# Turning over adjacency masks in a graph attention kernel: transposing transfers within SBUF in place of TensorE transposes and copies

## The chip, the cores and the metric

The kernel runs on one core of one Trainium2 chip. The metric is device time in microseconds (us) from the first to the last instruction; a kernel's time is the median of its runs. The profile shows one execution, on the engines TensorE (PE; its weight loads are listed as PEld), VectorE (DVE), ScalarE (ACT), GpSimd (POOL) and SyncE (SP, which here only issues transfers).

## The reference: what is computed

Two layers of graph attention over 32 graphs of 512 nodes with 512 features each. `adj` is an integer matrix of 512 x 512 per graph.

```python
# layer 0
h = relu(layernorm(x))
scores = leaky_relu(h@w_src [:, None] + h@w_dst [None, :] + b, 0.2)
scores = where(adj + eye == 0, -inf, scores)
x = x + softmax(scores, axis=-1) @ h                    # over the row of a node
# layer 1: two GAT layers, the first with 4 heads of 256, then elu, the second with 1 head of 512
h = relu(layernorm(x))
mask = (adj > 0) | eye
xl = (h @ W).reshape(B, N, H, F)
e = leaky_relu(asrc[:, :, None] + adst[:, None, :], 0.2)
attn = softmax(where(mask[..., None], e, -1e9), axis=1)  # over the column of a node
out = einsum('bsdh,bshf->bdhf', attn, xl) + bias
x = x + out
```

Everything is float32, and the masks are exact in bfloat16: an entry is 0 where there is an edge and -2^100 where there is none.

## The kernel before

A graph needs each of its two masks both ways: `m0` and its transpose `m0T` for layer 0, `m1` and `m1T` for the two attention layers of layer 1. One way is used by DVE to take the largest masked score of a row, the other is added to the scores by POOL ahead of the exponential. In layer 1 the maxima read `m1T` and the addition reads `m1`; in layer 0 the maxima read `m0` and the addition reads `m0T`.

```python
def edge_weights(kind, scores, a_of, c_of, mask_max, mask, junk_of=None):
    a_row = spread("m_row", scores + mask_max(*ROW), a_of, AHEAD)     # 4 TensorE transposes
    amax, z, m = Buffer("col"), Buffer("col"), Buffer("col")
    for t in range(T):                                                 # T = 4 blocks of 128 nodes
        def largest(t=t):
            nc.vector.tensor_tensor_reduce(                            # L480
                junk[...], mask_max.at[:, t, :], a_row.at, 1.0, LOWEST, ALU.add, ALU.max,
                accum_out=amax.at[:, t : t + 1])
        op("DVE", on_dve(N), largest, a_row(*ROW) + mask_max(t), amax(t))
    # ... cut: m from amax (L486, L488); m_row and c_row spread by TensorE (L417)
    for t in range(T):
        # ACT: E = Prelu(c_row + a)        L498
        # DVE: E = E - m_row               L501
        # POOL: E = E + mask               L503
        # ACT: E = exp(E)                  L506
    return E
```

The transposition of a mask, for which TensorE and a bfloat16 identity are used; a transpose lands in PSUM (kind "acc", four places), and ACT or DVE copies it to SBUF:

```python
def transposed_mask(m, mT, ahead):
    for k in range(T):
        pt = Buffer("acc")
        view = lambda pt=pt: pt.at[:, : N // 2].bitcast(BF16)
        for t in range(T):
            pe_transpose(                                              # L417
                ahead, pt, lambda t=t, view=view: view()[:, node_block(t)], m(t) + mT("place"),
                lambda t=t, k=k: m.at[:, t, node_block(k)], ident_b, t)
        evict(pt(*ROW), mT(k), view, lambda k=k: mT.at[:, k, :], N)    # L450 on ACT or L456 on DVE
```

Where the masks come from (`masks0` does the same for `m0`, with other comparisons), and the buffers concerned. There is one place for each of `adj`, `m0`, `m0T`, `m1` and `m1T`:

```python
def masks1(b):
    a, m1, m1T = load_adj(b), Buffer("m1"), Buffer("m1T")              # load on POOL's queue, L552
    op("DVE", ..., lambda: nc.vector.tensor_scalar(m1.at, a.at, 0.0, NO_EDGE, ...))    # L593
    for t in range(T):
        op("DVE", ..., lambda: nc.vector.tensor_mul(m1.at[:, t, own], ..., off_diag))  # L599
    transposed_mask(m1, m1T, AHEAD)
```

The products that project the features (L717) accumulate in PSUM places "sums" (two) and "acc" (four), and ACT or DVE copies or DVE adds (L450, L456, L730) the results to SBUF. The aggregation (L516) multiplies the weights E with the values.

All of this is laid out before the run by a planner: `op(engine, cost, emit, reads, writes, ahead)` records an operation, with how long it holds its engine and when its result is there (both in ns, as estimates written into the kernel), and `plan.run()` plays the operations through and emits them engine by engine in the order that comes out. Each engine then works in this fixed order. The estimates of the operations touched here:

```python
def on_pe(n, dtype=F32, transpose=False):
    if transpose:
        return (110.0, 300.0) if dtype == F32 else (68.0, 220.0)
    ...
def evict(...):  # ACT: n / 1.2 + 80 ns; DVE: n / 0.96 + 70 ns
```

The main loop, per graph b: masks and projection of layer 1, the end of graph b - 1, the four heads, layer 0 of the next graphs:

```python
for b in range(B + 1):
    if b < B:
        masks1(b)
        layer1_project(b)
    if b:
        load_back(b - 1)
        layer2_out(b - 1)
    # ... cut: load_x(b + 2)
    for h in range(H):
        Es.append(layer1_scores(b, h))        # edge_weights with m1T for the maxima
        # ... cut: layer1_head for the head before
    # ... cut: layer0_out(b + 1), layer1_in(b + 1), layer0_scores(b + 2) with masks0, layer2_project(b)
plan.run()
```

Of the kernel before, what the change touches and what calls it, by code (L numbers as in the profile page):

```python
# [9 lines left out]
F32 = mybir.dt.float32  # L10
BF16 = mybir.dt.bfloat16
# [4 lines left out]
P = 128  # L16
# [18 lines left out]
class Plan:  # L35
# [11 lines left out]
    def op(self, engines, cost, emit, reads=(), writes=(), ahead=0, lock=None):  # L47


        i = len(self.ops)  # L50
        after = set()
        for buf, part in reads:
            after.update(buf.wrote.get(part, ()))
        for buf, part in writes:
            after.update(buf.wrote.get(part, ()))
            after.update(buf.read.get(part, ()))
        bufs = []
        for buf, part in (*reads, *writes):
            if buf.kind is not None and buf not in bufs:
                bufs.append(buf)  # L60
                buf.left += 1
                if buf.left == 1 and buf.kind in self.turns:
                    self.turns[buf.kind].append(buf)
        for buf, part in reads:
            buf.read.setdefault(part, []).append(i)
        for buf, part in writes:
            buf.wrote[part] = [i]
            buf.read[part] = []
        after.discard(i)
        self.ops.append((engines if isinstance(engines, tuple) else (engines,), cost, emit, after, bufs, i - ahead, lock))  # L70
# [89 lines left out]
                    known(j)  # L160


def on_pe(n, dtype=F32, transpose=False):
    if transpose:
        return (110.0, 300.0) if dtype == F32 else (68.0, 220.0)
    one = 2 * max(0.8376 * n + 2, 110.0)
    return one, one + 170.0


def on_dve(n, speed=1.0, scaled_psum=False):  # L170
    one = n / 0.96 / speed + (130.0 if scaled_psum else 70.0)
    return one, one + 85.0


def on_act(n, per_partition=0):

    one = n / 1.2 + (80.0, 140.0, 280.0)[per_partition]
    return one, one + 60.0


def on_pool(n, narrow=False):
    one = 2.04 * n + 70.0 if narrow else 2.2 * n + 100.0
    return one, one + 30.0
# [3 lines left out]
def kernel(  # L187
# [24 lines left out]
    nc = tc.nc  # L212
    B, N, D = x.shape
    H, F = att_src1.shape
    HF = H * F
    T = N // P
# [8 lines left out]
    const = ctx.enter_context(tc.tile_pool(name="const", bufs=1))  # L225
# [9 lines left out]
    def node_block(t: int) -> slice:  # L235
        return slice(t * P, (t + 1) * P)
# [34 lines left out]
    op = plan.op  # L271


    ident = const.tile([P, P], F32, name="ident")
    make_identity(nc, ident)
    ident_b = const.tile([P, P], BF16, name="ident_b")
    nc.vector.tensor_copy(ident_b, ident)
    off_diag = const.tile([P, P], BF16, name="off_diag")
    nc.vector.tensor_scalar(off_diag, ident, 0.0, None, op0=ALU.is_equal)
    minus_half = const.tile([P, T], F32, name="minus_half")  # L280
# [131 lines left out]
    ROW = range(T)  # L412

    def pe_transpose(ahead, dst, dst_of, src, src_of, identity, part):

        dtype = BF16 if identity is ident_b else F32
        op("PE", on_pe(P, dtype, True), lambda: nc.tensor.transpose(dst_of(), src_of(), identity), src, dst(part), ahead)  # L417

    def layernorm(X):

# [25 lines left out]
    def evict(src, dst, src_of, dst_of, n, bias=None, psum_half=False):  # L446

        def by_act():
            if bias is None:
                nc.scalar.copy(dst_of(), src_of())  # L450
            else:
                nc.scalar.activation(dst_of(), src_of(), AF.Identity, bias=bias)  # L452

        def by_dve():
            if bias is None:
                nc.vector.tensor_copy(dst_of(), src_of())  # L456
            else:
                nc.vector.tensor_scalar(dst_of(), src_of(), -1.0, None, op0=ALU.add)

        op(("ACT", "DVE"), (on_act(n, bias is not None), on_dve(n)), (by_act, by_dve), src, dst)  # L460

    def spread(kind, part, col_of, ahead):

        row = Buffer(kind)
        for t in range(T):
            pe_transpose(
                ahead, row, lambda t=t: row.at[:, node_block(t)], part, lambda t=t: col_of(t).to_broadcast([P, P]), ident, t
            )
        return row

    AHEAD = 400

    def edge_weights(kind, scores, a_of, c_of, mask_max, mask, junk_of=None):

        a_row = spread("m_row", scores + mask_max(*ROW), a_of, AHEAD)
# [3 lines that stand above are left out]
                count[0] += 1  # L479
                nc.vector.tensor_tensor_reduce(  # L480
                    junk[count[0] % 2], mask_max.at[:, t, :], a_row.at, 1.0, LOWEST, ALU.add, ALU.max,
                    accum_out=amax.at[:, t : t + 1],
                )
            op("DVE", on_dve(N), largest, a_row(*ROW) + mask_max(t), amax(t))
        c_all = lambda: c_of(None)
        op("DVE", on_dve(T), lambda: nc.vector.tensor_add(z.at, c_all(), amax.at), scores + amax(*ROW), z(0))  # L486
        op(
            "DVE", on_dve(T), lambda: nc.vector.scalar_tensor_tensor(m.at, z.at, SLOPE, z.at, op0=ALU.mult, op1=ALU.max),  # L488
            z(0), m(0),
        )  # L490

        E = Buffer(kind)
        m_row = spread("m_row", m(0) + E("place"), lambda t: m.at[:, t : t + 1], AHEAD)
        c_row = spread("c_row", scores + E("place"), c_of, AHEAD)
        for t in range(T):
            op(
                "ACT", on_act(N, 1),
                lambda t=t: nc.scalar.activation(E.at[:, t, :], c_row.at, AF.Prelu, bias=a_of(t), scale=1.0, alpha=SLOPE),  # L498
                c_row(*ROW) + scores, E(t),
            )  # L500
            op("DVE", on_dve(N), lambda t=t: nc.vector.tensor_sub(E.at[:, t, :], E.at[:, t, :], m_row.at), m_row(*ROW) + E(t), E(t))  # L501
            op(
                "POOL", on_pool(N, True), lambda t=t: nc.gpsimd.tensor_add(E.at[:, t, :], E.at[:, t, :], mask.at[:, t, :]),  # L503
                E(t) + mask(t), E(t), lock=True,
            )
            op("ACT", on_act(N), lambda t=t: nc.scalar.activation(E.at[:, t, :], E.at[:, t, :], AF.Exp), E(t), E(t))  # L506
        return E
# [44 lines left out]
        op("POOL", (2200.0, 8000.0), lambda: nc.gpsimd.dma_start(a.at, node_tiles(adj, b)), (), a(0))  # L552
        return a

    def transposed_mask(m, mT, ahead):
        for k in range(T):
            pt = Buffer("acc")
            view = lambda pt=pt: pt.at[:, : N // 2].bitcast(BF16)
            for t in range(T):
                pe_transpose(  # L560
                    ahead, pt, lambda t=t, view=view: view()[:, node_block(t)], m(t) + mT("place"),
                    lambda t=t, k=k: m.at[:, t, node_block(k)], ident_b, t,
                )
            evict(pt(*ROW), mT(k), view, lambda k=k: mT.at[:, k, :], N)

    def masks0(b):


        a, m0, m0T, d = load_adj(b), Buffer("m0"), Buffer("m0T"), Buffer("d")
        op(  # L570
            "DVE", on_dve(T * N, 4.0),
            lambda: nc.vector.tensor_scalar(m0.at, a.at, 0.0, NO_EDGE, op0=ALU.is_equal, op1=ALU.mult),
            a(0), m0(*ROW), lock=True,
        )
        for t in range(T):
            own = node_block(t)
            op("DVE", on_dve(P), lambda t=t, own=own: nc.vector.tensor_add(d.at[:, t, :], a.at[:, t, own], ident), a(0), d(t), lock=True)
            op(
                "DVE", on_dve(P),
                lambda t=t, own=own: nc.vector.tensor_scalar(  # L580
                    m0.at[:, t, own], d.at[:, t, :], 0.0, NO_EDGE, op0=ALU.is_equal, op1=ALU.mult
                ),
                d(t), m0(t), lock=True,
            )
        transposed_mask(m0, m0T, AHEAD)
        return m0, m0T

    def masks1(b):

        a, m1, m1T = load_adj(b), Buffer("m1"), Buffer("m1T")  # L590
        op(
            "DVE", on_dve(T * N, 4.0),
            lambda: nc.vector.tensor_scalar(m1.at, a.at, 0.0, NO_EDGE, op0=ALU.is_le, op1=ALU.mult),  # L593
            a(0), m1(*ROW), lock=True,
        )
        for t in range(T):
            own = node_block(t)
            op(
                "DVE", on_dve(P), lambda t=t, own=own: nc.vector.tensor_mul(m1.at[:, t, own], m1.at[:, t, own], off_diag),  # L599
                m1(t), m1(t), lock=True,  # L600
            )
        transposed_mask(m1, m1T, AHEAD)
        M[b] = (m1, m1T)

    slots["d"] = places("d", 1, [P, T, P], BF16)
# [311 lines left out]
```

## Time and profile before

| | |
|---|---|
| time, median of 3 runs | 3947.34 us (3946.77 to 3950.04) |
| span of the profiled execution | 3948.1 us, mean granted TensorE clock 0.993 |
| busy: PE, DVE, ACT, POOL | 98%, 74%, 43%, 37% |
| DMA | 178.36 MB, mean 45 GB/s |
| time per graph in the steady part | some 120 us |

The page gives the busy time of each engine, the chain of work that ended last, and the groups of instructions by line. A group's line reads: line, engine, operation, output <- inputs by the program's names, shapes, count | busy us in total, mean ns of one | us that the engine sat idle just before them, and what ended that idle time. Matmuls are pipelined, so the mean time of one is longer than its share of TensorE's time. A float32 matmul shows up as two matmuls. A line of the view of waits reads: who <- waited for whom: us in total, times, longest. A line of the timeline reads: start in us, length in us, engine, line, operation, output <- inputs, shapes, how many are merged.

### The profile page before, as it was taken

The page shows a single profiled execution, that of the slowest core. Times are in us where ns is not written, and L with a number is a line of the kernel's source. Part 1 is how long each engine was busy: PE and PEld are TensorE (multiplying, and loading weights), DVE is VectorE, ACT ScalarE, POOL GpSimd, SP SyncE. Part 2 cuts the span into 40 slices and gives each one's busy share as a digit, 9 for nine tenths or more (in the row PEclk, how much of TensorE's full clock was granted, in tenths as well). Part 3 has the DMA queues.
Part 4 walks back from the last instruction along what each step waited for, and adds up shares of the span by engine and source line. Part 5 has one row for each costly group of instructions (what it writes and reads, how often), then busy time and mean ns, then how long its engine had stood idle before and what let it go on. Part 6 is the DMA issues. An engine that isn't in the chain of part 4 may idle for free.

```text
span 3948.1 us, 54741 instructions
## 1 busy us (share of the span) xinstructions
PE 3860.7 (98%) x20224; PEld 3342.0 (85%) x20224; DVE 2926.7 (74%) x7733; ACT 1715.3 (43%) x2991; POOL 1478.0 (37%) x1306
## 2 busy tenths in 40 slices
PE   4899999999999999999999999999999999999998
PEld 3788888888888888888888888888888888888887
DVE  6887767777777777777777677777777777777764
ACT  2444444444444454444444444444444544444432
POOL 3434333344333343343343433443343433433421
PEclk8999999999999999999999999999999999999999
DMA  4011111111111111111111111111111111111100
GB/s 136 6 54 54 33 49 49 33 54 52 30 49 54 33 54 33 49 49 33 54 54 33 47 50 33 54 44 37 49 48 39 54 33 49 49 33 54 49 22 22
DMA packets 107421, 178.36 MB, mean 45 GB/s; under 512 B 3728, under 2 KB 40592, under 8 KB 107152
## 3 DMA queue, kind: packets, MB, share of 16 engines
q1 hardware_dynamic: 72064, 138.42, 9.5%
q0 software_dynamic: 33792, 33.56, 5.4%
q8 instruction: 158, 2.59, 0.3%
q10 hardware_dynamic: 1296, 2.88, 0.2%
q14 instruction: 111, 0.91, 0.1%
HBM read 141.30 MB, written 67.11 MB: 53 GB/s over the span
## 4 chain that ended last, share of the span: by engine, by line
PE 96%; DVE 2%; DMA 1%; POOL 1%; issue 1%; ACT 0%; SPq 0%; DVEq 0%; ACTq 0%; POOLq 0%
PE acc L516 45%; PE sums L717 22%; PE acc L717 17%; PE acc L417 6%; PE m_row L417 4%; PE c_row L417 2%; DVE junk L307 1%; POOL E_one L503 1%; DMA w<-in_L_gnn_W_dram 0%; DVE E_one L501 0%; ACT E_one L506 0%; DVE junk L480 0%; DMA x<-in_x_dram 0%; DMA w_T<-in_L_gnn_W_dram 0%; DVE w_T L399 0%
## 5 line engine op out<-in xcount | busy, mean ns | idle before, releaser
L516 PE MATMUL acc<-pair,E 128*128 128x257 f32 x4096 | 913.2, 380 | 0.0
L503 POOL TENSOR_TENSOR E<-E,m 128x512 f32<-128x512 f32 x512 | 577.6, 1157 | 825.3 <-DVE E L501 818.3
L516 PEld LDWEIGHTS acc<-pair,E 128*128 128x128 f32 x4096 | 769.2, 189 | 119.2 <-ACT pair L452 5.5
L516 PE MATMUL acc<-h,E_one 128*128 128x256 f32 (+1 forms) x2048 | 501.6, 384 | 6.3 <-ACT E_one L506 3.9
L791 ACT ACTIVATE e<-v,minus_one 128x512 f32<-128x512 f32 x256 | 184.7, 722 | 717.8 <-DVE v L782 682.4
L516 PE MATMUL acc<-xl,E_one 128*128 128x257 f32 (+1 forms) x2048 | 479.5, 381 | 2.7 <-ACT E_one L506 2.7
L480 DVE CUSTOM_DVE_ANT_0 junk<-m1T,m_row 128x512 bf16<-128x512 bf16 x640 | 411.1, 682 | 51.5 <-PE m_row L417 50.9
L506 ACT ACTIVATE E<-E 128x512 f32<-128x512 f32 x512 | 323.6, 632 | 229.6 <-POOL E L503 227.8
L516 PEld LDWEIGHTS acc<-xl,E_one 128*128 128x128 f32 x2048 | 378.6, 190 | 51.8 <-ACT E_one L506 3.1
L516 PEld LDWEIGHTS acc<-h,E_one 128*128 128x128 f32 x2048 | 367.1, 191 | 55.6 <-ACT E_one L506 13.8
L501 DVE TENSOR_TENSOR E<-E,m_row 128x512 f32<-128x512 f32 x512 | 330.3, 679 | 14.7 <-PE m_row L417 12.2
L498 ACT ACTIVATE E<-c_row,pair 128x512 f32<-128x512 f32 x512 | 314.6, 690 | 48.6 <-PE c_row L417 47.7
L717 PE MATMUL acc<-w_T,E 128*128 128x257 f32 (+1 forms) x1024 | 268.1, 384 | 14.7 <-DVE x L534 14.7
L794 DVE SCALAR_TENSOR_TENSOR v<-e,v 128x512 f32<-128x512 f32 x256 | 177.7, 694 | 138.8 <-ACT e L791 134.6
L534 DVE SCALAR_TENSOR_TENSOR x<-acc,r,x 128x256 f32<-128x256 f32 x512 | 244.8, 479 | 46.3 <-PE acc L516 43.7
L717 PE MATMUL sums<-w_T,E 128*128 128x257 f32 (+1 forms) x1024 | 271.6, 381 | 0.0
L717 PE MATMUL acc<-w,E 128*128 128x257 f32 (+1 forms) x1024 | 264.6, 381 | 0.0
L503 POOL TENSOR_TENSOR E_one<-E_one,m0T 128x512 f32<-128x512 f32 x128 | 146.5, 1176 | 309.8 <-DVE E_one L501 309.8
L506 ACT ACTIVATE E_one<-E_one 128x512 f32<-128x512 f32 x256 | 161.3, 630 | 232.1 <-POOL E_one L503 228.9
L782 DVE SCALAR_TENSOR_TENSOR v<-acc,r,b_r 128x256 f32<-128x256 f32 x512 | 246.2, 481 | 13.7 <-DVE r L779 0.4
L779 DVE RECIPROCAL r<-acc 128x1 f32<-128x1 f32 x512 | 83.5, 163 | 214.1 <-PE acc L516 211.5
L503 POOL TENSOR_TENSOR E_one<-E_one,m 128x512 f32<-128x512 f32 x128 | 144.3, 1160 | 234.1 <-DVE E_one L501 234.1
(123 smaller groups left out, 6750.1 us busy)
## 6 DMA issues: line engine op xcount, KB each, us to landing
x<-in_x_dram SPq DMA_DIRECT2D x32, 1024.0 KB, 5.1
adj<-in_adj_dram POOLq DMA_DIRECT2D x64, 512.0 KB, 5.8
spill<-x SPq DMA_DIRECT2D x32, 1024.0 KB, 4.3
x<-spill SPq DMA_DIRECT2D x32, 1024.0 KB, 5.7
out_dram<-x SPq DMA_DIRECT2D x32, 1024.0 KB, 4.3
w<-in_L_gnn_W_dram SPq DMA_DIRECT2D x6, 256.0 KB, 9.0
w<-in_L_gnn_W_dram SPq DMA_DIRECT2D x8, 127.5 KB, 4.9
w_T<-in_L_gnn_W_dram SPq DMA_DIRECT2D x4, 128.5 KB, 5.8
```

What stands on the lines that cost most here:

```text
L417: op("PE", on_pe(P, dtype, True), lambda: nc.tensor.transpose(dst_of(), src_of(), identity), src, dst(part), ahead)
L480: nc.vector.tensor_tensor_reduce(junk[count[0] % 2], mask_max.at[:, t, :], a_row.at, 1.0, LOWEST, ALU.add, ALU.max, accum_out=amax.at[:, t ...
L498: lambda t=t: nc.scalar.activation(E.at[:, t, :], c_row.at, AF.Prelu, bias=a_of(t), scale=1.0, alpha=SLOPE),
L501: op("DVE", on_dve(N), lambda t=t: nc.vector.tensor_sub(E.at[:, t, :], E.at[:, t, :], m_row.at), m_row(*ROW) + E(t), E(t))
L503: "POOL", on_pool(N, True), lambda t=t: nc.gpsimd.tensor_add(E.at[:, t, :], E.at[:, t, :], mask.at[:, t, :]),
L506: op("ACT", on_act(N), lambda t=t: nc.scalar.activation(E.at[:, t, :], E.at[:, t, :], AF.Exp), E(t), E(t))
L516: lambda s=s: nc.tensor.matmul(acc.at[:, :n], E.at[:, s, node_block(t)], of(s), start=(s == 0), stop=(s == T - 1)),
L534: lambda acc=acc, r=r, f=f, t=t: nc.vector.scalar_tensor_tensor(X.at[:, t, f], acc.at[:, :HD], r.at, X.at[:, t, f], op0=ALU.mult, op1=ALU. ...
L717: lambda k=k: nc.tensor.matmul(acc.at[:, :width], at[a]()[:, k, node_block(r)], weight_of(w, k, c), start=(first and k == 0), stop=(k == n ...
L782: lambda t=t, acc=acc, r=r: nc.vector.scalar_tensor_tensor(v.at[:, t, :], acc.at[:, :F], r.at, b1_r[:, h * F : (h + 1) * F], op0=ALU.mult, ...
L791: op("ACT", on_act(2 * F, 1), lambda e=e, ts=ts: nc.scalar.activation(e.at, v.at[:, ts, :], AF.Exp, bias=minus_one), parts, e(0))
L794: lambda e=e, ts=ts: nc.vector.scalar_tensor_tensor(v.at[:, ts, :], e.at, 1.0, v.at[:, ts, :], op0=ALU.min, op1=ALU.max),
```

## The change

The transposes of both masks are made by transposing transfers from SBUF to SBUF, issued on SyncE's queue, four for each mask. Transfer t reads the block of 128 rows t of the mask, 128 x 512 in bfloat16 (128 KB), and writes the column strip t of all four blocks of the transpose. TensorE's bfloat16 transposes, their copies out of PSUM and the bfloat16 identity are dropped. The aim is to free TensorE, and ACT and DVE, of work that a transfer can do.

Since each transfer writes a strip across all blocks, the maxima for one row block, and likewise the addition by POOL, now depend on all four transfers. The planner is told that a transfer holds the queue for 100 ns and lands after 3500 ns.

```diff
-def on_pe(n, dtype=F32, transpose=False):
+def on_pe(n, transpose=False):
     if transpose:
-        return (110.0, 300.0) if dtype == F32 else (68.0, 220.0)
+        return 110.0, 300.0
 ...
-    ident_b = const.tile([P, P], BF16, name="ident_b")
-    nc.vector.tensor_copy(ident_b, ident)
 ...
-            op("DVE", on_dve(N), largest, a_row(*ROW) + mask_max(t), amax(t))
+            op("DVE", on_dve(N), largest, a_row(*ROW) + mask_max(*ROW), amax(t))
 ...
-                E(t) + mask(t), E(t), lock=True,
+                E(t) + mask(*ROW), E(t), lock=True,
 ...
-    def transposed_mask(m, mT, ahead):
-        for k in range(T):
-            pt = Buffer("acc")
-            view = lambda pt=pt: pt.at[:, : N // 2].bitcast(BF16)
-            for t in range(T):
-                pe_transpose(
-                    ahead, pt, lambda t=t, view=view: view()[:, node_block(t)], m(t) + mT("place"),
-                    lambda t=t, k=k: m.at[:, t, node_block(k)], ident_b, t,
-                )
-            evict(pt(*ROW), mT(k), view, lambda k=k: mT.at[:, k, :], N)
+    def transposed_mask(m, mT):
+        for t in range(T):
+            op(
+                "SP", (100.0, 3500.0),
+                lambda t=t: nc.sync.dma_start(mT.at[:, :, node_block(t)], m.at[:, t, :], transpose=True),
+                m(t), mT(t),
+            )
```

More of the change, by code (lines that the diff above doesn't have):

```diff
@@ L414, in pe_transpose @@
     def pe_transpose(ahead, dst, dst_of, src, src_of, identity, part):
-        dtype = BF16 if identity is ident_b else F32
-        op("PE", on_pe(P, dtype, True), lambda: nc.tensor.transpose(dst_of(), src_of(), identity), src, dst(part), ahead)
+        op("PE", on_pe(P, transpose=True), lambda: nc.tensor.transpose(dst_of(), src_of(), identity), src, dst(part), ahead)
     def layernorm(X):
@@ L584, in masks0 @@
             )
-        transposed_mask(m0, m0T, AHEAD)
+        transposed_mask(m0, m0T)
         return m0, m0T
@@ L601, in masks1 @@
             )
-        transposed_mask(m1, m1T, AHEAD)
+        transposed_mask(m1, m1T)
         M[b] = (m1, m1T)
```

## The prediction

> **What bounds the kernel now.** I read the busy shares first, then the chain that ended last, to see whether the busiest engine is also the one that sets the end.
>
> ```profile
> PE 3860.7 (98%) x20224; PEld 3342.0 (85%) x20224; DVE 2926.7 (74%) x7733; ACT 1715.3 (43%) x2991; POOL 1478.0 (37%) x1306
> ...
> PE 96%; DVE 2%; DMA 1%; POOL 1%; issue 1%; ACT 0%; SPq 0%; DVEq 0%; ACTq 0%; POOLq 0%
> ```
>
> TensorE is both. So an instruction taken off TensorE is worth its place in TensorE's queue, and one taken off VectorE (DVE) or ScalarE (ACT) is worth nothing by itself, unless TensorE was waiting for it. The view of waits for TensorE shows how little it waits:
>
> ```profile
> PE m_row L417 <- DVE col L488: 18.3, 3, 14.2
> PE acc L417 <- DVE m L580: 18.0, 3, 16.4
> PE acc L717 <- DVE x L534: 14.7, 1, 14.7
> ```
>
> The longest single waits (14.2, 16.4 and 14.7 us) make up most of each sum, so they are events of the start and the end, not of the 120 us that each of the 32 graphs takes in between. Next the instructions that the change removes, by group:
>
> ```profile
> L417 PE MATMUL acc<-ident_b,m 128*128 128x128 bf16 x1024 | 78.0, 220 | 19.1 <-DVE m L580 18.0 <-DVE x L534 0.7 <-ACT m1T L450 0.3
> L450 ACT COPY m0T<-acc 128x512 bf16<-128x512 bf16 x67 | 35.4, 579 | 9.2 <-PE acc L417 9.2
> L450 ACT COPY m1T<-acc 128x512 bf16<-128x512 bf16 x65 | 34.9, 589 | 37.2 <-PE acc L417 35.4
> L456 DVE COPY m1T<-acc 128x512 bf16<-128x512 bf16 x63 | 25.5, 423 | 28.0 <-PE acc L417 28.0
> L456 DVE COPY m0T<-acc 128x512 bf16<-128x512 bf16 x61 | 24.1, 417 | 14.8 <-PE acc L417 14.8
> ```
>
> 1,024 transposes (32 graphs x 2 masks x 16 blocks), 132 copies on ACT, 124 on DVE. Last, how the turned mask m1T is used in one steady graph; this is the timeline of all engines from 1546 us on:
>
> ```profile
> 1546.16 0.62 DVE L599 TENSOR_TENSOR m<-m,off_diag 128x128 bf16<-128x128 bf16 x4
> ...
> 1546.68 0.83 PE L417 MATMUL acc<-ident_b,m 128*128 128x128 bf16 x12
> ...
> 1547.35 1.09 PE L717 MATMUL sums<-w_-T,hT 128*128 128x258 f32 x4
> ...
> 1550.50 0.69 DVE L480 CUSTOM_DVE_ANT_0 junk<-m1T,m_row 128x512 bf16<-128x512 bf16 x1 [1.31 <-PE m_row L417]
> ...
> 1559.13 3.38 POOL L503 TENSOR_TENSOR E<-E,m 128x512 f32<-128x512 f32 x3 [12.11 <-DVE E L501]
> ```
>
> The mask is finished at 1546.8 us, turned over by 1549.2, and first read by DVE at 1550.5 (row maxima of head 0). So the consumer comes 3.7 us behind the mask: that is the deadline which a transfer has to meet.
>
> **What the Trainium skill says.** "VectorE: DVE Perf Modes", section "The three transpose paths", puts a 128x128 bf16 transpose at 390 ns on TensorE and 1309 ns on the DMA crossbar. On TensorE the trace has 220 ns for one and, as worked out below, one each 56 ns in a row, so the page's time is one of latency; whether its 1309 ns is latency or rate no run here shows yet, and the two readings are my rivals. "Advanced Engine Details and Errata", section "X-Bar Transpose (TRN2)", says transposing transfers are as fast as others (350 to 400 GB/s); "DMA: Bandwidth & Descriptors", section "Latency and other measured facts", has 261 GB/s where the middle dimension isn't contiguous, which is the case in this destination. The kernel before has no such transfer. "TensorE: Matmul & The Clock Gate", section "Part 4: PE-mode transpose", says that the result lands in PSUM and needs a copy: the trace agrees (the 256 copies above).
>
> **The change, part by part.**
>
> *Removed from TensorE.* Not the busy time of 78.0 us: the last matmul's pipeline tail lies under the next one. The cost is start to start. In the lines above the first of 12 transposes starts at 1546.68 and the next product at 1547.35: 0.67 / 12 = 56 ns. The same difference over all the runs of transposes between 120 and 3660 us gives 55.4 us for 944, over the last 32 1.8 us. The first 48 lie in the start, where TensorE is idle two thirds of the time and they cost nothing. Gain: **57 us**. The 18.0 us of waiting in front of the transposes isn't gained: 16.4 of it is the very first wait, at 16.4 us, and the next TensorE work waits for DVE until 21.4 us anyhow.
>
> *Removed from ACT and DVE.* 70 us of ACT and 50 us of DVE, and 8 uses of the four "acc" PSUM places per graph. TensorE hardly waits for either in the steady part, so I put 0 there. In the start (60 to 120 us) DVE is busy 58.4 of 60 us; six of its copies at 0.42 us are some **2 us**.
>
> *Added.* 256 transfers of 128 KB on SyncE's queue, 33.5 MB in all beside 178 MB now; the DMA engines have a share of 11 to 15%, so bandwidth is no matter. SyncE issues four transfers per graph today (a store, a load, a store, a load), and holds 0.36 us for one; ordinary 1 MB transfers land in 4.3 to 5.7 us.
>
> *What becomes late.* m0T isn't pressed: m0 is done at 1567.6 us and m0T is read at 1650.8, 83 us later. m1T is: the maxima for row block 0 read one column strip from each of the four transfers, so the first of them waits for the last transfer. The kernel's own planner lays out all queues before the run; it takes a transfer to hold SyncE for 100 ns and to land after 3500 ns. Four then land by 0.3 + 3.5 = 3.8 us after the mask, and with signals and the m_row transposes it puts the first maximum some 4.7 us after the mask (before: 3.7). The engines work in that fixed order. If the transfers land later, DVE stands at that maximum, with the copies and additions behind it that empty PSUM for TensorE's products.
>
> *How much of such a stall reaches TensorE.* A product of four matmuls takes 0.87 us; TensorE has 6 PSUM places, and its next product into the same place waits for the copy. I estimate that it runs on for about two products, 2 us. DVE can't catch up soon: between 1552 and 1563.5 us it is busy 11.43 of 11.5. So each us of stall beyond 2 costs about 1 us, times 32. The chain behind the maxima itself has room: head 0's weights are ready 17 us after the mask and first used at 33.6.
>
> So: time = 3947 - 57 - 2 + 32 x max(0, landing - 4.7 - 2) + a little at the start, where SyncE also issues the weights.
>
> **The rivals.**
>
> A, *hidden*: 1309 ns is mostly latency, and a transfer behaves like the others, 0.4 us of SyncE each. Four land in 4 to 5 us. 3947 - 59 + 2 = **3890**. For it: the low DMA share, and the planner's 3.5 us, which was probably taken from a run, since its 5.5 us for the x load lies near the measured 5.1. Weight 0.35.
>
> B, *queued one behind another*: a transfer lands in 3.5 us, but holds the queue for 1.2 to 1.5 us, about what the page has for one block. The last lands at 3.5 + 3 x 1.4 = 7.7 us; DVE stands 3 us, TensorE 1 us: +32, and some 4 us at the start, where x and the weights queue behind. 3888 + 36 = **3924**. Weight 0.38. Against it nothing in this profile; it has no such transfer.
>
> C, *rate*: 1309 ns for every 128x128 block, one behind another. Sixteen blocks take 21 us; DVE stands at the maxima for 16 us, TensorE for 14: +450 us, **4335**; with half that time per block (10.5 us for four), +120, about 4010. Against it: the section on the crossbar, and that the planner would hardly have been left with 3.5 us. Weight 0.27.
>
> A further way, better than A, would need TensorE to lose something now to PSUM places or copies; the waits above show none of it, so more than 2% (below 3868) needs 79 us where I find 59.
>
> **Range and chances.** The middle of the weights lies between A and B, towards B: **3912 us**. The low end is A with a few us more from freed PSUM places, 3878; the high end reaches into the milder half of C, 4130. Below 3868: 0.06. Above 4026: most of C, with a little of B, 0.28. Between: 0.66.
>
> **What would show it.** In the profile after: the group of bf16 transposes and the m0T and m1T copies gone; TensorE's busy time lower by about 75 us (it counts tails). Time from issue to landing of the new transfers, and how far apart SyncE issues the four: 0.4 us is A, over 1 us B, over 3 us C. In the waits, DVE at the maxima (L480) waiting for a DMA: none in A, about 3 us x 32 in B, over 5 us x 32 in C; and TensorE's idle time before the products, for the copies or additions that DVE does late. POOL should not wait for m0T. I would be wrong if the planner's new order alone moves TensorE's waits by tens of us, if SyncE at the head of its queue holds up loads of x, or if TensorE can stand a longer stall of DVE than 2 us.

## The result, and the profile after

| | before | changed |
|---|---|---|
| time, median | 3947.82 us | 4086.39 us |
| ratio to before, 95% interval | | 1.0353 [1.0335, 1.037] |
| span profiled, mean granted clock | 3948.1 us, 0.993 | 4084.2 us, 0.982 |
| from one mask m1 to the next, mean of graphs 2 to 30 | 119.96 us | 124.14 us |

The changed kernel is 3.5% slower. Of the page of the changed kernel, the lines that answer to those shown before: the busy shares, the chain that ended last by engine, and the two groups of transfers that have come in (output <- input, engine, operation, count, median us from issue to landing).

```profile
PE 3851.2 (94%) x19200; PEld 3318.6 (81%) x19200; DVE 2922.4 (72%) x7605; ACT 1640.8 (40%) x2859; POOL 1478.6 (36%) x1309
...
PE 86%; DVE 8%; DMA 4%; issue 1%; ACT 1%; POOL 1%; SPq 0%; DVEq 0%; ACTq 0%; POOLq 0%
...
m0T<-m SPq DMA_TRANSPOSE x128, 2.4
m1T<-m SPq DMA_TRANSPOSE x128, 5.9
```

TensorE has 1,024 instructions fewer and idles more: its share fell from 98% to 94%, and the chain now runs through DVE and the transfers. The two kinds of transfer are the same in size and form, but m1T's take 5.9 us to land and m0T's 2.4. Who waits is told by the view of waits over all engines and, in the last two lines, that of TensorE alone:

```profile
DVE junk L477 <- DMA m1T<-m: 129.3, 31, 6.5
```

```profile
PE sums L711 <- DVE pair L724: 107.3, 31, 5.4
...
PE m_row L414 <- DVE col L477: 21.1, 14, 1.5
```

DVE waits for m1T at the maxima (L477 here, L480 before) 31 times, 4.2 us on average, and TensorE in its turn waits 31 times for DVE's additions out of PSUM (L724). Neither wait was in the kernel before. One of them in full, from the timeline of the changed kernel, from the mask of one graph on (in brackets, how long the engine had been idle just before, and what ended that):

```profile
1605.40 0.63 DVE L593 TENSOR_TENSOR m<-m,off_diag 128x128 bf16<-128x128 bf16 x4
1605.66 5.83 SPq L556 DMA_TRANSPOSE m1T<-m  x4
...
1605.67 0.82 POOL L549 DMA_DIRECT2D adj<-in_adj_dram  x1 [1.21 <-DVE m L593]
...
1610.00 0.43 DVE L724 TENSOR_TENSOR pair<-acc,pair 128x258 f32<-128x258 f32 x1 [0.44 <-PE acc L711]
...
1611.98 0.60 PE L711 MATMUL acc<-w_T,E 128*128 128x258 f32 x2
...
1615.16 0.69 DVE L477 CUSTOM_DVE_ANT_0 junk<-m1T,m_row 128x512 bf16<-128x512 bf16 x1 [4.74 <-DMA m1T<-m]
...
1615.78 0.42 DVE L724 TENSOR_TENSOR pair<-sums,pair 128x258 f32<-128x258 f32 x1
...
1616.26 2.09 PE L711 MATMUL sums<-w_-T,hT 128*128 128x258 f32 x4 [3.68 <-DVE pair L724]
```

SyncE is 5.83 us about the four transfers. Beside them GpSimd starts the load of the next adjacency matrix, whose place the mask has just set free. DVE's last addition ends at 1610.4; the next thing in its order is the first maximum, and it stands until 1615.16. TensorE runs on until 1612.6, then waits 3.68 us for a PSUM place that an addition has to empty. When it starts again, four matmuls take 2.09 us where four otherwise take 1.03 in this timeline. The view by windows gives the granted clock for the stretch before the stall, the stall, and the two after it. A line reads: stretch in us, its length, then the busy us (and instructions) of PE, PEld, DVE, ACT and POOL, the granted TensorE clock (1.00 is full speed), the mean busy share of the DMA engines, and the GB/s they moved:

```profile
1606.00:1612.40 6.40, 6.40 (x35) 5.40 (x33) 1.31 (x4) 3.39 (x7) 0.49 (x1) 1.00 1.21 120
1612.40:1616.26 3.86, 0.18 (x2) 0.01 (x1) 1.10 (x4) 0.15 (x1) 0.00 (x0) 0.96 0.41 74
1616.26:1618.00 1.74, 1.74 (x4) 1.46 (x5) 1.74 (x7) 0.00 (x0) 0.00 (x0) 0.50 0.00 0
1618.00:1622.00 4.00, 4.00 (x18) 3.34 (x18) 3.02 (x14) 1.12 (x3) 0.00 (x0) 0.83 0.17 33
```

After the stall TensorE runs at half speed.

### The profile page after: what moved, and what is told of

It is laid out like the page before. It is cut to its first block, busy times and chain, and to the rows that moved or that the text cites. A ratio compares the mean times of both kernels' runs of the same rounds, so it can differ in the third digit from the quotient of the medians.

```text
span 4084.2 us, 52936 instructions
## 1 busy us (share of the span) xinstructions
PE 3851.2 (94%) x19200; PEld 3318.6 (81%) x19200; DVE 2922.4 (72%) x7605; ACT 1640.8 (40%) x2859; POOL 1478.6 (36%) x1309
## 3 DMA queue, kind: packets, MB, share of 16 engines
q10 hardware_dynamic: 1296, 2.88, 0.2%
## 4 chain that ended last, share of the span: by engine, by line
PE 86%; DVE 8%; DMA 4%; issue 1%; ACT 1%; POOL 1%; SPq 0%; DVEq 0%; ACTq 0%; POOLq 0%
PE acc L513 40%; PE sums L711 20%; PE acc L711 16%; PE acc L414 4%; PE m_row L414 4%; DMA m1T<-m 3%; PE c_row L414 2%; DVE E L498 2%; DVE junk L477 1%; DVE junk L305 1%; DVE m L574 1%; DMA w<-in_L_gnn_W_dram 1%; DVE x L531 1%; DVE pair L724 1%; POOL E_one L500 0%
## 5 line engine op out<-in xcount | busy, mean ns | idle before, releaser
L477 DVE CUSTOM_DVE_ANT_0 junk<-m1T,m_row 128x512 bf16<-128x512 bf16 x640 | 413.0, 681 | 180.4 <-DMA m1T<-m 129.3
L447 ACT COPY pair<-sums 128x258 f32<-128x258 f32 x305 | 114.0, 374 | 451.0 <-PE sums L711 448.9
L711 PE MATMUL acc<-w_T,E 128*128 128x257 f32 (+1 forms) x1024 | 278.5, 392 | 11.8 <-DVE x L531 11.7
L711 PE MATMUL sums<-w_-T,hT 128*128 128x258 f32 x512 | 153.7, 421 | 107.3 <-DVE pair L724 107.3
```

The costliest lines, as they stand in the source:

```text
L477: nc.vector.tensor_tensor_reduce(junk[count[0] % 2], mask_max.at[:, t, :], a_row.at, 1.0, LOWEST, ALU.add, ALU.max, accum_out=amax.at[:, t ...
L711: lambda k=k: nc.tensor.matmul(acc.at[:, :width], at[a]()[:, k, node_block(r)], weight_of(w, k, c), start=(first and k == 0), stop=(k == n ...
```

## The experiments

Theory L, as it stood before the runs: the planner lays out DVE's order for a landing 3.8 us after the mask, the last m1T transfer lands 9 us after it, DVE stands at the first maximum in between with TensorE's additions behind it, and the clock falls. Rival P: the planner's new order, without transposes and copies, fits worse whatever the transfers do. Rival S: the transfers slow other work through shared DMA engines or SBUF. Below, "stand" is DVE's idle time just before the first maximum of head 0, a mean of graphs 2 to 29; so is the start of that maximum after the mask.

**Nothing turned over.** The maxima and the additions read the mask itself; both transpositions are left out, so the output isn't that of the reference.

```diff
-        transposed_mask(m0, m0T)
-        return m0, m0T
+        return m0, m0
-        transposed_mask(m1, m1T)
-        M[b] = (m1, m1T)
+        M[b] = (m1, m1)
```

> The masks aren't turned over at all: the maxima and the additions read the mask itself, so neither TensorE transposes nor transfers are there. Theory L (the changed kernel loses its time because DVE stands at the first maximum of head 0 until the last m1T transfer has landed, TensorE runs out of PSUM places behind it, and its clock is halved for 3.4 us afterwards): about 3888 us, 59 below the kernel before, since nothing is waited for. Rival P (the planner's order without the transposes and copies fits worse, whatever the transfers do): above 3947, towards 4080. Rival S (the transfers slow other work by sharing DMA engines or SBUF): 3888 as well.

Measured: 3910.89 us, ratio 0.9905 [0.9888, 0.9921]. Below the kernel before, so removing the work does help; but 23 us above what L and S put, which is a share for rival P. In this order, without any landing to wait for, TensorE waits for an addition 15 times, 1 us each (15.2 us). P is real, then, with some 20 us in this order, not 140. The order of the changed kernel is another one, and this run doesn't tell P's share there.

**Only m0T, and only m1T, by transfers**, the other by TensorE as before. In both, the maxima and the additions depend on all four parts of a mask, as in the changed kernel.

```diff
-        transposed_mask(m0, m0T, AHEAD)
+        sent_mask(m0, m0T)        # the four transfers; in the second kernel the same for m1, m1T only
```

> Half of the change: only m0T is made by transfers, m1T by TensorE as before. Theory L: m0T isn't read for some 80 us, so nothing waits; half of the TensorE time is gained, 28 us, about 3919. Rival S: half of the extra time of the changed kernel is there, about 3947 - 28 + 98 = 4017. Rival P: between 3919 and 4017.

> The other half: only m1T is made by transfers, m0T by TensorE as before. Theory L: all of the loss is here and half of the gain is missing: 4086 + 28 = about 4114. Rival S: about 4017, as for the other half.

Measured: m0T alone 3925.59 us, 0.9942 [0.9927, 0.9957]; m1T alone 4126.82 us, 1.0453 [1.0435, 1.0471]. 128 transfers of the same size gain 22 us in the one place and lose 179 in the other. Rival S falls: both halves send the same bytes. It is the place in the schedule that counts.

**The planner is told the truth.** The kernel and its transfers stay, two numbers change:

```diff
-                "SP", (100.0, 3500.0),
+                "SP", (1300.0, 5500.0),
```

> The changed kernel, but the planner is told what the trace shows: a transfer holds SyncE's queue for 1300 ns (was 100) and lands after 5500 (was 3500), so that the last of four lands 9.4 us after the mask instead of 3.8. Theory L: the planner puts copies and additions ahead of the first maximum, DVE hardly stands, TensorE's clock stays up: 3890 to 3910. If the maxima are simply needed by then and the chain behind them is short of time: 3950 to 4050. Rivals P and S: about 4086, as the transfers are the same.

Measured: 3890.4 us, 0.9852 [0.9837, 0.9867]. That is 196 us from two estimates. The transfers are no faster, as the page of this kernel shows, and the maxima (group line, with what ended the idle time before them) hardly wait for them:

```profile
L477 DVE CUSTOM_DVE_ANT_0 junk<-m1T,m_row 128x512 bf16<-128x512 bf16 x640 | 413.7, 681 | 40.3 <-PE m_row L414 34.0
...
m1T<-m SPq DMA_TRANSPOSE x128, 6.1
```

The first maximum now begins 10.25 us after the mask, later than in the changed kernel (8.85), and costs nothing: the stand is 0.49 us instead of 4.20, since DVE's order has the additions, and the next m0 mask, in front of it. The timeline of this kernel, DVE only:

```profile
1531.45 0.63 DVE L593 TENSOR_TENSOR m<-m,off_diag 128x128 bf16<-128x128 bf16 x4
1534.38 0.43 DVE L724 TENSOR_TENSOR pair<-acc,pair 128x258 f32<-128x258 f32 x1 [2.30 <-PE acc L711]
...
1536.99 0.43 DVE L724 TENSOR_TENSOR pair<-sums,pair 128x258 f32<-128x258 f32 x1 [0.51 <-PE sums L711]
1539.75 0.69 DVE L566 TENSOR_SCALAR m<-adj 128x2048 bf16<-128x2048 bf16 x1 [2.33 <-DMA adj<-in_adj_dram]
...
1542.15 0.69 DVE L477 CUSTOM_DVE_ANT_0 junk<-m1T,m_row 128x512 bf16<-128x512 bf16 x1
```

**Two wrong estimates more**, one between and one beyond: (1300, 3500), and (100, 2000).

> The planner is told only the hold of the queue (1300 ns), the landing stays at 3500: it then expects the last of four 7.4 us after the mask and puts the first maximum at 8 or later, where the trace has 9.1. Theory L: DVE stands about 1 us, which TensorE's PSUM places cover: 3890 to 3905. If TensorE loses every us that DVE stands: about 3890 + 31 = 3921.

> The planner is told a landing of 2000 ns instead of 3500 (hold 100 ns as in the changed kernel), so that the first maximum comes 1.5 us earlier in DVE's order. Theory L: DVE and TensorE stand 1.5 us longer in each graph, 4086 + 31 x 1.5 = about 4132. Rival P (any order without the transposes is as good or bad as another): anything between 3950 and 4100, with no reason to be longer.

Measured: 3919.33 us, 0.9929 [0.9913, 0.9946], and 4121.73 us, 1.0437 [1.0422, 1.0453]. A later planned maximum loses less and an earlier one more. Stands of 0.49, 0.96, 4.20 and 7.29 us go with 3890, 3919, 4086 and 4122 us. The small stand is not free: 0.47 us more per graph went with 29 us, 5 of them before graph 2, the rest 0.8 us per graph (118.58 for 117.77). TensorE waits there 17 times, 17.0 us in all, for the result of the maxima, which its transposes for m_row need; PSUM places, on which my first number for this run rested, don't cover that wait.

The last 3.1 us of stand cost only 36 us. TensorE waits there once in each graph, for the result of the maxima (157.6 us in 31 waits), and no longer for the additions. Between 240 and 3660 us it runs 164 us at half speed (89 in the changed kernel), but 46 of them (6 in the changed kernel) fall into its own idle time, where they cost no work. Idle time and the work lost to the clock together make 7.4 us per graph more than in the kernel told the truth, and 7.4 are measured (125.17 for 117.77); for the changed kernel the same sum is made below.

**The adjacency load later.** The plan makes it depend on head 0's weights, so that it goes out behind GpSimd's additions for head 0.

```diff
-            (), a(0))                      # load_adj, on GpSimd's queue
+            behind, a(0))
-            layer0_scores(b + 2)
+            layer0_scores(b + 2, Es[0](0))
```

> The changed kernel with its estimates as they are, but the load of the next adjacency matrix, which now starts beside the four m1T transfers, is put behind the additions of head 0 on GpSimd's queue. Theory L with contention: alone the last transfer lands some 6.1 us after the mask, as in the last graph of the changed kernel, which has no such load; DVE stands under 2 us, TensorE about 1 us a graph and its clock stays up: 3890 + 31 x 1 = about 3920. If the four transfers hold up one another and the load has no part in it: about 4086.

> Both edits: the planner told 1300 and 5500 ns, and the adjacency load behind the additions of head 0. With the load later alone the m1T transfers landed in 2.5 us, yet 4043 us were measured where 3920 was expected, with new waits of TensorE for x and v from DVE. If those came from an order laid out with too short estimates: about 3890 here. If the later load itself pushes the m0 mask and the maxima of layer 0 into a stretch where DVE has no room: above 3930.

Measured: 4042.86 us with the estimates as they were, 1.024 [1.0225, 1.0256]; 3894.68 us with the planner told, 0.9861 [0.9846, 0.9875]. The page of the first, landing of m0T and m1T:

```profile
m0T<-m SPq DMA_TRANSPOSE x128, 5.0
m1T<-m SPq DMA_TRANSPOSE x128, 2.5
```

m1T's was 5.9 in the changed kernel: the load beside them is what more than doubles the landing. The load now runs beside m0T's transfers, and theirs went from 2.4 to 5.0. The last of the four for m1T still comes 6.3 us after the mask (8.6 in the changed kernel, both means of graphs 2 to 29), since each holds the queue; the first maximum comes 6.48 us after the mask and the stand falls to 1.83 us. But the time fell by 44 us and not by 166 as I expected. From TensorE's waits in this kernel, and in the last line DVE's:

```profile
PE acc L513 <- DVE x L531: 49.5, 29, 2.5
PE sums L711 <- DVE pair L724: 37.6, 31, 3.6
...
PE acc L414 <- DVE v L788: 29.3, 33, 1.9
```

```profile
DVE st L420 <- DMA x<-in_x_dram: 119.5, 31, 12.3
```

TensorE's wait for the additions went from 107.3 to 37.6 us; two new ones of 49.5 and 29.3 took its place. The last line shows what is behind them: DVE stands at the statistics of the next x until x has been loaded, 29 times in the steady part, 3.4 us on average, with those operations behind it; in the changed kernel it does so only twice, in the first 40 us (17.5 us). From the fourth load of x on, each follows the store of the output on SyncE's queue there; here each follows an m0T transfer and takes some 7.6 us to land instead of 5.3 (medians). So a second thing became late, and it is one that the prediction had named as a sign of being wrong: SyncE holding up the loads of x. These waits are gone when the planner is told true estimates, with the same adjacency load in the same place (for x DVE again waits twice only, 17.5 us). So they belong to the order that the short estimates gave, and not to the later load by itself. And with the planner told, the collision no longer matters: 3895 without it, 3890 with it.

**A second place for m1**, estimates as they were; then both remedies.

```diff
-        "m1": places("m1", 1, [P, T, N], BF16),
+        "m1": places("m1", 2, [P, T, N], BF16),
```

> The changed kernel with its estimates as they are, but two places for m1 instead of one. The mask of the next graph no longer waits for the last addition of this one, so the transfers can start as soon as the last maxima have read m1T, some 9 us earlier, and land ahead of the planned maximum. Theory L (the wait is for the landing): 3885 to 3910. If the maxima follow the mask as closely as before because the planner moves them forward as well: 4000 to 4086.

> The two remedies together: the planner told 1300 and 5500 ns, and two places for m1. Each alone took DVE's wait for the transfers away and came to 3890 and 3894 us. If that wait was all there was to gain, the two together are no better: 3885 to 3895. If the start, where TensorE waits for DVE for some 8 us more than before, is also a matter of the estimates or of m1's place: 3875 to 3885.

Measured: 3893.66 us, 0.9859 [0.9845, 0.9874]; together 3885.63 us, 0.9838 [0.9822, 0.9854]. With two places the mask no longer waits for the last reader of the one before and is made a whole graph ahead, 118 us before its first maximum. m1T still has one place, so the transfers go out when the last maxima have read the m1T before, 7.3 us ahead of the first maximum. The adjacency load is no longer beside them: they land in 2.5 us (median), the last one 0.6 us before the first maximum begins, where the planner with its wrong estimates has put it (DVE waited 2.2 us in all for m1T). So this edit changes both the wait and the company of the transfers. The two remedies together are the best version here, 64 us below the kernel before and 201 below the changed one. In it DVE stands 2.2 us at the first maximum, for TensorE's m_row and never for a transfer, and TensorE is busy for 3419.87 of the 3420 us from 240 to 3660 us: here a stand costs time only where TensorE waits behind it.

## Why the prediction was wrong

**The bound, and what was removed: right.** TensorE's time is what counted. Told the truth, the kernel gained 57 us, the figure of the prediction, though by another sum: the graphs of the steady part gained 2.19 us each (119.96 to 117.77; the prediction's 55.4 us for 944 transposes are 1.88 for the 32 of a graph), and the start, up to graph 2's mask, took 7 us more (354.1 for 347.2), where I had put 2 us of gain. This start is much the same in "nothing turned over" (355.4), so SyncE's transfers aren't its cause; with m1T alone by transfers it is not there (348.7), so it goes with m0T leaving TensorE. What of the order costs the 7 us stays open, and so do the 0.3 us per graph. TensorE's busy time fell by 74 us in the kernel told the truth (3860.7 to 3786.8, 75 predicted), but only by 9.5 in the changed one, where matmuls at half speed take longer.

**What becomes late: right in place.** m1T and not m0T, DVE standing at the first maximum of head 0, additions out of PSUM behind it, as in rival B.

**The rivals.** The queue is held 1.24 us (median) for an m1T transfer; with no load beside it a transfer lands in 2.4. Rival C (16 blocks one behind another, 21 us) is excluded: the last of the four lands 8.6 us after the mask. Of A only that such a transfer is quick was true. So B holds, with 8.6 us for its landing of 7.7 and 4.2 us for its stand of 3.

**The step that failed** is "how much of such a stall reaches TensorE". The prediction took 2 us off every stand and charged the rest once, 1 us per graph in B. In the changed kernel a graph takes 6.4 us longer than in the kernel told the truth. In all B put 36 us (32 of stall, 4 at the start) where 198 were lost (4086 - 3888). The late landing alone would not have done it: with 8.6 us the prediction's formula loses 32 x (8.6 - 4.7 - 2) = 61 us, about what the removed work gains. Term by term:

- *The landing*, 0.9 us later than in B. I had looked at the DMA engines' mean share (11 to 15%) and called bandwidth no matter; in the few us that count, the transfers run beside the adjacency load, which the same mask releases. Both the load and the engines' share just behind the mask (0.65) were there to see before the change, in its timeline and its view by windows:

```profile
1546.21 0.82 POOL L552 DMA_DIRECT2D adj<-in_adj_dram  x1 [1.03 <-DVE m L593]
```

```profile
1546.77:1552.00 5.23, 5.23 (x41) 4.62 (x40) 2.69 (x8) 4.20 (x8) 0.26 (x1) 1.00 0.65 103
```

- *The 2 us that TensorE runs on.* It does run on for some 2 us (1610.4 to 1612.6 in the graph shown). But I took them off the loss, and they aren't gained: TensorE starts again only 1.1 us after DVE's stand has ended (1615.16 to 1616.26), with a maximum and an addition in between, and what DVE didn't do in the stall it had to do afterwards, with TensorE waiting a second time (the 14 waits for L477's result). Over 240 to 3660 us the windows of the changed kernel and of the one told the truth are

```profile
240.00:3660.00 3420.00, 3292.22 (x16500) 2841.56 (x16499) 2483.35 (x6438) 1406.05 (x2448) 1252.05 (x1111) 0.99 0.22 52
```

```profile
240.00:3660.00 3420.00, 3416.86 (x17423) 2968.00 (x17422) 2569.57 (x6761) 1509.92 (x2614) 1318.33 (x1160) 1.00 0.25 54
```

  TensorE is idle 127.8 us against 3.1, in 27.5 graphs 4.5 us more each, for 3.7 us more of DVE's standing.
- *The clock*, not in the sum at all. In the trace's clock record the changed kernel runs 89 us of the same stretch at half speed, 6 of them while it is idle; the other 83 cost 41 us of work, 1.5 us per graph. The kernels before and told the truth have no such time there.

Together 4.5 + 1.5 = 6.0 us per graph; measured are 124.14 - 117.77 = 6.4. On the kernel told the truth that makes 3890 + 31 x 6.0 = 4076, against 4086 measured, so little is left over. The number of the prediction, 3912, was a middle between A and B, but the direction was not lost there: B itself, 3924, was still faster than the kernel before. With the measured terms it is slower.

**The planner's 3.5 us** I took as probably measured and as evidence for A. Where it comes from no run tells, and evidence for A it was not: a transfer took 2.4 us with no load beside it and 5.9 with one, and the 100 ns for the queue were wrong by a factor of 12.

## What to carry to other kernels

In a kernel whose engines work in an order fixed beforehand, a late result costs not only its own wait but everything queued behind the waiter; look for what stands behind the first reader. When work moves to another unit, give the planner that unit's time as it is in the place of use (four in a row, with the load that starts at the same moment), or give the data another place so that it can be made early. And check a transfer's company in the few us around its deadline; a mean share over the run says nothing of it.

## What the runs showed of the hardware that I had not expected

- A transposing transfer of 128 x 512 bf16 within SBUF holds its queue for at least 1.19 us, where an ordinary transfer of 1 MB holds it for 0.36. It lands in 2.4 us (median of m0T) where no such load is beside it, and in 5.9 us (median of m1T, up to 9.3) as one of four beside a load of 512 KB that converts integers to bf16. In the changed kernel the first of the four lands 0.27 us after that load has, the last 1.56 (medians of graphs 2 to 29), as if they waited for it; why isn't shown.
- A pause of TensorE of about 3 us can cost clock. The Trainium skill, "TensorE: Matmul & The Clock Gate", section "Why this matters for your kernels", warns of gaps over some 3 us between bursts; the trace agrees in the main, with no sharp edge. Between 240 and 3660 us of the changed kernel no drop followed where two matmuls began up to 1.91 us apart; between 2.88 and 3.16 us one followed in 4 of 10 cases; from 3.28 us on it followed in all 18, at half speed for 3.4 us, and for 6.8 us after the four longest (4.81 us and more). Elsewhere less was enough: 2.51 us at 185 us in the same kernel, 2.72 us in the one with the adjacency load later.
